# Block products for graph convolution: fewer PSUM banks per set of seven, partial sums copied out between the products

## The chip, the cores and the metric

The kernel runs on one core of a Trainium2 chip. The metric is device time in microseconds (us). The kernel before takes 2972.11 us, the median of three runs (2971.57 to 2972.21).

The engines are named as the profile names them. PE is TensorE, which multiplies matrices into PSUM; PEld is its loading of weights. DVE is VectorE, ACT is ScalarE and POOL is GpSimd. PSUM has eight banks here, each of 128 partitions by 512 float32 values. GpSimd works on SBUF tiles only in this kernel.

## The reference, cut to what matters

There are 64 graphs of 256 nodes with 512 features. Layer 0 is three graph convolutions, with a residual and a layer norm. Layer 1 is an attention without a full score matrix: one score for each node, a softmax over the nodes, and again a residual and a layer norm.

```python
# layer 0, for each graph
h = relu(adj @ (x @ W1) + b1)
h = relu(adj @ (h @ W2) + b2)
x = layernorm(x + adj @ (h @ W3) + b3)
# layer 1
q, k = split(x @ Wqk);  v = x @ Wv
agg = adj @ (k * mask)
w = mask * sum(q * agg, -1) / sqrt(512)
x = layernorm(x + softmax(w over nodes) * v)
```

Everything is float32.

## The kernel before

The kernel works on pairs of graphs (32 pairs). It has two streams of work that are emitted in turn: `front` does the first two convolutions of pair i, `back` the third convolution and the attention of pair i-1. `back` has more steps than `front`, so the last part of `back` is emitted when `front` of that turn has ended.

Most products (the three of features by weights, two with the adjacency, and one for each graph in the attention) use a scheme with seven block products in place of eight. Operands are cut into 2 x 2 blocks; sums and differences of blocks are made first, seven products are formed, and the four result blocks are sums of these. The products are numbered: 1 to 4 use plain blocks on at least one side, 5, 6 and 7 use sums on both. In the attention, q and k are folded into one matrix, M = Wq Wk^T, made once at the start.

The function that runs one set of seven:

```python
def seven(mm, c11, c12, c21, c22, shape, add11=None, plus=None):
    a = bank(shape)
    mm(1, a, True)                  # True: the first product in this bank
    t1 = tmp()...                   # [cut: a reshape]
    nc.scalar.copy(t1, a)           # ScalarE
    yield
    b = bank(shape)
    mm(6, b, True)
    u = tmp()...
    add(u, b, t1)                   # VectorE
    if plus is not None:            # only where the residual is added
        u12, u21, u22 = (tmp()... for _ in range(3))
        padd(u22, u, plus[2])       # GpSimd
        padd(u12, u, plus[0])
        padd(u21, u, plus[1])
    else:
        u12 = u21 = u22 = u
    yield
    c = bank(shape)
    mm(7, c, True)
    s7 = tmp()...
    add(s7, c, u22)
    yield
    d = bank(shape)
    mm(5, d, True)
    c22(d, s7)
    yield
    mm(2, a, False)                 # False: adds to what the bank holds
    c11(a)
    yield
    mm(3, d, False)
    c12(d, u12)
    yield
    mm(4, c, False)
    c21(c, u21)
    yield
```

Each `yield` hands the turn to the other stream. The sums of blocks of the features, made by GpSimd. `S[0]` goes to product 5, `S[1]` to 6, `S[2]` to 7, `S[3]` to 3:

```python
def a_sums(hT):                     # hT: four chunks of 128 features
    S = [pool.tile([P, 2, G, P], FP, name="S", tag="S", bufs=6) for _ in range(4)]
    blk = lambda h, c: hT[c][:, :, h * P:(h + 1) * P]
    sub = OP.subtract
    for c in range(2):
        padd(S[0][:, c], blk(1, c), blk(1, 2 + c))
    for c in range(2):
        padd(S[1][:, c], S[0][:, c], blk(0, c), sub)
    for c in range(2):
        padd(S[2][:, c], blk(0, c), blk(1, c), sub)
    for c in range(2):
        padd(S[3][:, c], blk(0, 2 + c), S[1][:, c], sub)
    ...                             # [cut: which source each product takes]
```

The features by weights (`support`), and the two streams:

```python
def support(hT, w):
    src = a_sums(hT)
    C = ...                         # [cut: four tiles for the result blocks]
    ...                             # [cut: mm(n, ps, first), 4 matmuls of 256 columns]
    yield from seven(mm, lambda a: nc.scalar.copy(C[0][0], a), lambda d, u: add(C[0][1], d, u),
                     lambda c, u: add(C[1][0], c, u), lambda d, u: add(C[1][1], d, u), (P, G, HD))
    return C

def front(i, hT, aT):
    C = yield from support(hT, wl[0])
    nxt = load_xT(i + 1) if i + 1 < NPAIR else None
    hT = yield from aggregate(C, aT, bcol[0])     # four steps, relu on ScalarE after each
    C = yield from support(hT, wl[1])
    hT = yield from aggregate(C, aT, bcol[1])
    return hT, nxt

def back(i, hT, aT, prev):
    # [cut: load of x, softmax and end of the pair before]
    C = yield from src                            # src = support(hT, wl[2])
    aS = adj_sums(aT)
    # [cut]
    yield from adj_times(aS, C, ..., plus=(xb(0, 1), xb(1, 0), xb(1, 1)))   # into r, with x
    for g in range(G):
        layernorm(r[:, g])
    yield 8
    # [cut: 16 transposes of r into x1T; mask times r into xm, on ScalarE]
    src = a_sums(x1T)
    # [cut: attention(g), a set of seven with products of 512 columns]
    yield from adj_times(aS, xmb, ...)            # into gt
    for g in range(G):
        yield from attention(g)
    return r, vs, w
```

`adj_times` makes four sums T of the other operand on GpSimd and then runs `seven` with products of two matmuls each. A float32 matmul shows as two records in the profile, so a product of `support` has eight records.

Of the kernel before, what the change touches and what calls it, by code (L numbers as in the profile page):

```python
# [20 lines left out]
def gcn_then_graph_attention(ctx: ExitStack, tc: tile.TileContext, xT, xN, adjT, mask, W1, b1, W2, b2, W3, b3,  # L21
# [29 lines left out]
    def bank(shape=(P, G, N)):  # L51
        return psum.tile(list(shape), FP, name="ps", tag="ps")

    def tmp():
        return pool.tile([P, D], FP, name="tmp", bufs=5)

    def add(o, a, b):
        nc.vector.tensor_tensor(o, a, b, op=OP.add)  # L58

    def padd(o, a, b, op=OP.add):  # L60
        nc.gpsimd.tensor_tensor(o, a, b, op=op)  # L61


    def load_xT(i):
        t = pool.tile([P, DC, G, N], FP, name="xT", bufs=1)
        nc.sync.dma_start(t, xT[i].rearrange("p (c g n) -> p c g n", c=DC, g=G))
        return [t[:, c] for c in range(DC)]

    def load_adj(i):
        t = pool.tile([P, NH, G, N], FP, name="aT", bufs=2)  # L70
# [17 lines left out]
    def halves(t, w):  # L88
        return t[:, :w], t[:, w:]

    def seven(mm, c11, c12, c21, c22, shape, add11=None, plus=None):

        a = bank(shape)
        mm(1, a, True)
        t1 = tmp().rearrange("p (a b) -> p a b", a=shape[1]) if len(shape) == 3 else tmp()
        nc.scalar.copy(t1, a)  # L96
        yield
        b = bank(shape)
        mm(6, b, True)
        u = tmp().rearrange("p (a b) -> p a b", a=shape[1]) if len(shape) == 3 else tmp()  # L100
        add(u, b, t1)
        if plus is not None:
            u12, u21, u22 = (tmp().rearrange("p (a b) -> p a b", a=shape[1]) for _ in range(3))
            padd(u22, u, plus[2])
            padd(u12, u, plus[0])
            padd(u21, u, plus[1])
        else:
            u12 = u21 = u22 = u
        yield
        c = bank(shape)  # L110
        mm(7, c, True)
        s7 = tmp().rearrange("p (a b) -> p a b", a=shape[1]) if len(shape) == 3 else tmp()
        add(s7, c, u22)
        yield
        d = bank(shape)
        mm(5, d, True)
        c22(d, s7)
        yield
        mm(2, a, False)
        c11(a)  # L120
        yield
        mm(3, d, False)
        c12(d, u12)
        yield
        mm(4, c, False)
        c21(c, u21)
        yield


# [38 lines left out]
    def make_m():  # L168

        qk = []  # L170
        for name, w, tag, in (("q", WqT, "act"), ("k", WkT, "sup")):
            qk.append([])
            for d in range(DC):
                t = pool.tile([P, D], FP, name=f"w{name}T", tag=tag, bufs=7)
                nc.sync.dma_start(t, w[d * P:(d + 1) * P, :])
                qk[-1].append(t)
        m = [const.tile([P, 2, D], FP, name=f"m{k}") for k in range(2)]
        v0 = pool.tile([P, 2, D], FP, name="v0", tag="v", bufs=3)
        nc.sync.dma_start(v0, Wv[:HD].rearrange("(c p) f -> p c f", p=P))
        v1 = const.tile([P, 2, D], FP, name="v1")  # L180
        nc.sync.dma_start(v1, Wv[HD:].rearrange("(c p) f -> p c f", p=P))
        yield
        for f in range(DC):
            pt = bank((P, D))
            for d in range(DC):
                nc.tensor.matmul(pt, lhsT=qk[0][d][:, f * P:(f + 1) * P], rhs=qk[1][d],
                                 start=(d == 0), stop=(d == DC - 1))
            nc.scalar.copy(m[f // 2][:, f % 2, :], pt)
            yield
        ts = [const.tile([P, 2, D], FP, name=f"mv_{s}") for s in KEYS]  # L190
        b_sums((m[0], v0, m[1], v1), ts, nc.gpsimd)
        mv.update({1: m[0], 2: m[1], 3: v1, 4: ts[3], 5: ts[0], 6: ts[1], 7: ts[2]})
        yield


    def a_sums(hT):

        S = [pool.tile([P, 2, G, P], FP, name="S", tag="S", bufs=6) for _ in range(4)]
        blk = lambda h, c: hT[c][:, :, h * P:(h + 1) * P]
        sub = OP.subtract  # L200
        for c in range(2):
            padd(S[0][:, c], blk(1, c), blk(1, 2 + c))
        for c in range(2):
            padd(S[1][:, c], S[0][:, c], blk(0, c), sub)
        for c in range(2):
            padd(S[2][:, c], blk(0, c), blk(1, c), sub)
        for c in range(2):
            padd(S[3][:, c], blk(0, 2 + c), S[1][:, c], sub)
        src = {1: lambda c, g: blk(0, c)[:, g], 2: lambda c, g: blk(0, 2 + c)[:, g],
               4: lambda c, g: blk(1, 2 + c)[:, g]}  # L210
        for n, s in ((5, 0), (6, 1), (7, 2), (3, 3)):
            src[n] = lambda c, g, s=s: S[s][:, c, g]
        return src

    def support(hT, w):

        src = a_sums(hT)
        C = [[pool.tile([P, G, HD], FP, name="sup", tag="sup", bufs=7) for _ in range(2)] for _ in range(2)]

        def mm(n, ps, first):  # L220
            for g in range(G):
                for c in range(2):
                    nc.tensor.matmul(ps[:, g], lhsT=src[n](c, g), rhs=w[n][:, c], start=(first and g == 0 and c == 0),  # L223
                                     stop=(g == G - 1 and c == 1), skip_group_check=True)
        yield from seven(mm, lambda a: nc.scalar.copy(C[0][0], a), lambda d, u: add(C[0][1], d, u),
                         lambda c, u: add(C[1][0], c, u), lambda d, u: add(C[1][1], d, u), (P, G, HD))
        return C

    def aggregate(C, aT, b):

        hT = []
        for c in range(DC):
            ps = bank()
            for g in range(G):
                for k in range(NH):
                    nc.tensor.matmul(ps[:, g], lhsT=C[k][c // 2][:, g, (c % 2) * P:(c % 2 + 1) * P],  # L236
                                     rhs=aT[:, k, g], start=(g == 0 and k == 0), stop=(g == G - 1 and k == NH - 1),
                                     skip_group_check=True)
            t = pool.tile([P, G, N], FP, name="hT", tag="act", bufs=7)
            nc.scalar.activation(t, ps, AF.Relu, bias=b[:, c:c + 1])  # L240
            hT.append(t)
            yield
        return hT

# [10 lines left out]
    def adj_times(aS, B, c11, c12, c21, c22, plus=None):  # L255

        Ts = [pool.tile([P, G, HD], FP, name="T", tag="T", bufs=4) for _ in range(4)]
        b_sums((B[0][0], B[0][1], B[1][0], B[1][1]), Ts, nc.gpsimd)
        mov = {1: B[0][0], 2: B[1][0], 3: B[1][1], 4: Ts[3], 5: Ts[0], 6: Ts[1], 7: Ts[2]}

        def mm(n, ps, first):
            for g in range(G):
                nc.tensor.matmul(ps[:, g], lhsT=aS[n][:, g], rhs=mov[n][:, g], start=(first and g == 0),  # L263
                                 stop=(g == G - 1), skip_group_check=True)
        yield from seven(mm, c11, c12, c21, c22, (P, G, HD), plus=plus)

    def stats(src):

# [50 lines left out]
    def back(i, hT, aT, prev):  # L319
# [10 lines left out]
        if prev is not None:  # L330
            s = softmax_cols(sm)
            for g in range(G):
# [3 lines left out]
        r = pool.tile([P, G, NH, D], FP, name="r", bufs=2)  # L336
        xb = lambda h, j: x[:, :, h, j * HD:(j + 1) * HD]
        rb = lambda h, j: r[:, :, h, j * HD:(j + 1) * HD]
        yield from adj_times(aS, C, lambda a: add(rb(0, 0), a, xb(0, 0)), lambda d, u: add(rb(0, 1), d, u),
                             lambda c, u: add(rb(1, 0), c, u), lambda d, u: add(rb(1, 1), d, u),  # L340
                             plus=(xb(0, 1), xb(1, 0), xb(1, 1)))
        for g in range(G):
            layernorm(r[:, g])
        yield 8
        x1T = []
        for c in range(DC):
            pt = bank()
            for g in range(G):
                for h in range(NH):
                    nc.tensor.transpose(pt[:, g, h * P:(h + 1) * P], r[:, g, h, c * P:(c + 1) * P], ident)  # L350
            t = pool.tile([P, G, N], FP, name="x1T", bufs=4)
            if c % 2:
                nc.vector.tensor_copy(t, pt)
            else:
                nc.scalar.copy(t, pt)
            x1T.append(t)
        yield
        xm = pool.tile([P, G, NH, D], FP, name="xm", tag="x", bufs=1)
        for h in range(NH):
# [10 lines left out]
        def attention(g):  # L370
# [10 lines left out]
                nc.vector.scalar_tensor_tensor(prod, y, mask_s[:, h, b:b + 1], gt[:, h, g, :], op0=OP.mult,  # L381
                                               op1=OP.mult, accum_out=w[:, h, g:g + 1])

            def c21(c, u):
                y = tmp()
                add(y, c, u)
                score(y, 1)
            vs[g] = v
            yield from seven(mm, lambda a: score(a, 0), lambda d, u: add(v[:, 0, :], d, u), c21,
                             lambda d, u: add(v[:, 1, :], d, u), (P, D))  # L390
        yield from adj_times(aS, xmb, lambda a: nc.scalar.copy(gb(0, 0), a), lambda d, u: add(gb(0, 1), d, u),
                             lambda c, u: add(gb(1, 0), c, u), lambda d, u: add(gb(1, 1), d, u))
        for g in range(G):
            yield from attention(g)
        return r, vs, w
# [79 lines left out]
```

## Time and profile before

| | |
|---|---|
| median of three runs | 2972.11 us |
| span of the profiled run | 2969.8 us |
| ScalarE busy | 623.7 us (21%) |
| GpSimd busy | 1413.6 us (48%) |
| one sum S of 128x256 on GpSimd | 0.73 us |
| one sum T of 128x512 on GpSimd | 1.27 us |
| one copy of a bank by ScalarE | 0.58 us |
| one addition of a bank by VectorE | 0.69 us |
| granted TensorE clock, mean | 0.994 |

An engine's busy time is the union of the stretches in which it ran something. An idle stretch is put down to the instruction, on whatever engine, whose end let the waiting one start. In the lists below, a group reads: line of the kernel, engine, operation, tile written <- tiles read, shape, count. A group's times are its busy time, the mean of one, and the idle time before it with its releasers. A line number can be that of a helper: L58 is VectorE's addition, L61 GpSimd's, L96 the copy of `t1`, L223 the matmuls of `support`, L236 those of `aggregate`, L263 those of `adj_times`, L376 those of the attention.

### The profile page before, as it was taken

The page shows a single profiled execution, that of the slowest core. Times are in us where ns is not written, and L with a number is a line of the kernel's source. Part 1 is how long each engine was busy: PE and PEld are TensorE (multiplying, and loading weights), DVE is VectorE, ACT ScalarE, POOL GpSimd, SP SyncE. Part 2 cuts the span into 40 slices and gives each one's busy share as a digit, 9 for nine tenths or more (in the row PEclk, how much of TensorE's full clock was granted, in tenths as well). Part 3 has the DMA queues.
Part 4 walks back from the last instruction along what each step waited for, and adds up shares of the span by engine and source line. Part 5 has one row for each costly group of instructions (what it writes and reads, how often), then busy time and mean ns, then how long its engine had stood idle before and what let it go on. Part 6 is the DMA issues. An engine that isn't in the chain of part 4 may idle for free. (4 is left out here: it accounts for less than half of the span.)

```text
span 2969.8 us, 30813 instructions
## 1 busy us (share of the span) xinstructions
PE 2882.4 (97%) x11680; PEld 2156.5 (73%) x11680; DVE 1356.8 (46%) x2638; ACT 623.7 (21%) x1062; POOL 1413.6 (48%) x1642
## 2 busy tenths in 40 slices
PE   7999999999999999999999999999999999999996
PEld 5877777777778777777777787777777777877774
DVE  2344544444444445444444444454444444444545
ACT  1212222212222122222122221222121222211221
POOL 5445455344554454554445544545544455445452
PEclk8999999999999999999999999999999999999998
DMA  4001011011011010110110110101101101101000
GB/s 146 31 34 50 26 46 50 29 50 50 22 50 49 31 50 29 43 50 29 50 50 22 50 50 29 50 30 41 50 29 50 50 22 50 50 29 50 33 17 29
DMA packets 28724, 126.04 MB, mean 42 GB/s; under 512 B 3232, under 2 KB 6432, under 8 KB 20384
## 3 DMA queue, kind: packets, MB, share of 16 engines
q1 hardware_dynamic: 28576, 124.08, 11.4%
q8 instruction: 92, 1.51, 0.2%
q14 instruction: 56, 0.46, 0.0%
HBM read 90.51 MB, written 33.55 MB: 42 GB/s over the span
## 5 line engine op out<-in xcount | busy, mean ns | idle before, releaser
L58 DVE TENSOR_TENSOR tmp<-ps,tmp 128x512 f32<-128x512 f32 x512 | 353.4, 690 | 693.9 <-PE ps L376 281.3
L223 PE MATMUL ps<-w_T,S 128*128 128x256 f32 x2304 | 538.1, 383 | 50.3 <-POOL S L61 50.2
L223 PEld LDWEIGHTS ps<-w_T,S 128*128 128x128 f32 x2304 | 434.4, 191 | 122.0 <-POOL S L61 63.1
L236 PE MATMUL ps<-aT,sup 128*128 128x256 f32 x2048 | 473.8, 381 | 0.0
L236 PEld LDWEIGHTS ps<-aT,sup 128*128 128x128 f32 x2048 | 386.4, 190 | 61.8 <-DVE sup L58 10.6
L376 PE MATMUL ps<-mv_T,S 128*128 128x512 f32 x768 | 340.0, 592 | 0.0
L96 ACT COPY tmp<-ps 128x512 f32<-128x512 f32 x224 | 130.3, 581 | 922.7 <-PE ps L376 464.7
L58 DVE TENSOR_TENSOR sup<-ps,tmp 128x512 f32<-128x512 f32 x288 | 194.4, 684 | 221.5 <-PE ps L223 116.6
L240 ACT ACTIVATE hT<-ps,b 128x512 f32<-128x512 f32 x256 | 175.9, 687 | 548.9 <-PE ps L236 548.9
L376 PEld LDWEIGHTS ps<-mv_T,S 128*128 128x128 f32 x768 | 145.9, 190 | 183.7 <-issue 160.7
L61 POOL TENSOR_TENSOR S<-hT 128x256 f32<-128x256 f32 x256 | 181.7, 725 | 204.7 <-PE ps L223 171.8
L83 POOL TENSOR_TENSOR T<-sup 128x512 f32<-128x512 f32 x32 | 40.6, 1269 | 426.2 <-DVE sup L58 426.2
L223 PE MATMUL ps<-w,hT 128*128 128x256 f32 x1024 | 242.0, 379 | 0.0
L376 PE MATMUL ps<-m,x1T 128*128 128x512 f32 x512 | 240.6, 592 | 0.0
L223 PEld LDWEIGHTS ps<-w,hT 128*128 128x128 f32 x1024 | 192.1, 190 | 25.7 <-issue 0.3
L83 POOL TENSOR_TENSOR T<-xm 128x512 f32<-128x512 f32 x32 | 40.8, 1274 | 326.9 <-ACT xm L362 320.1
L263 PE MATMUL ps<-T,aS 128*128 128x256 f32 x768 | 187.8, 381 | 1.4 <-POOL T L84 1.4
L275 ACT ACTIVATE sd<-mv,eps 128x2 f32<-128x2 f32 x128 | 34.5, 292 | 701.6 <-DVE mv L273 701.6
L223 PE MATMUL ps<-w,S 128*128 128x256 f32 x768 | 181.3, 379 | 0.1
L376 PEld LDWEIGHTS ps<-m,x1T 128*128 128x128 f32 x512 | 97.3, 190 | 108.8 <-issue 107.2
L61 POOL TENSOR_TENSOR S<-xT 128x256 f32<-128x256 f32 x128 | 90.8, 731 | 167.3 <-PE ps L376 160.7
L263 PEld LDWEIGHTS ps<-T,aS 128*128 128x128 f32 x768 | 146.8, 191 | 22.1 <-POOL T L84 1.8
(93 smaller groups left out, 3932.1 us busy)
## 6 DMA issues: line engine op xcount, KB each, us to landing
xT<-in_xT SPq DMA_DIRECT2D x32, 1024.0 KB, 4.9
x<-in_xN SPq DMA_DIRECT2D x32, 1024.0 KB, 4.9
out<-v SPq DMA_DIRECT2D x64, 512.0 KB, 2.6
aT<-in_adjT SPq DMA_DIRECT2D x32, 512.0 KB, 5.4
w<-in_W SPq DMA_DIRECT2D x9, 256.0 KB, 5.3
wqT<-in_WqT SPq DMA_DIRECT2D x4, 256.0 KB, 5.2
wkT<-in_WkT SPq DMA_DIRECT2D x4, 256.0 KB, 5.0
v<-in_Wv SPq DMA_DIRECT2D x2, 512.0 KB, 6.4
```

Of the source, the lines that this page charges most:

```text
L58: nc.vector.tensor_tensor(o, a, b, op=OP.add)
L61: nc.gpsimd.tensor_tensor(o, a, b, op=op)
L83: eng.tensor_tensor(Ts[0], B[1], B[0], op=sub)
L96: nc.scalar.copy(t1, a)
L223: nc.tensor.matmul(ps[:, g], lhsT=src[n](c, g), rhs=w[n][:, c], start=(first and g == 0 and c == 0), stop=(g == G - 1 and c == 1), skip_gr ...
L236: nc.tensor.matmul(ps[:, g], lhsT=C[k][c // 2][:, g, (c % 2) * P:(c % 2 + 1) * P], rhs=aT[:, k, g], start=(g == 0 and k == 0), stop=(g == ...
L240: nc.scalar.activation(t, ps, AF.Relu, bias=b[:, c:c + 1])
L263: nc.tensor.matmul(ps[:, g], lhsT=aS[n][:, g], rhs=mov[n][:, g], start=(first and g == 0), stop=(g == G - 1), skip_group_check=True)
L275: nc.scalar.activation(sd, mvt[:, :, 1], AF.Sqrt, bias=eps)
L376: nc.tensor.matmul(ps, lhsT=src[n](c, g), rhs=mv[n][:, c], start=(first and c == 0), stop=(c == 1), skip_group_check=True)
```

## The change: three banks, copies between the products, sums of half the features

What it does:

- `seven` takes its products in the order 1, 7, 6, 2, 5, 3, 4 and uses three banks, x, v and y. Products 1, 6, 5 and 3 gather in x: after 1, after 6 and after 5 ScalarE copies what the bank holds, and the next product is added on top. Products 7 and 4 gather in v; product 2 has y for itself. What VectorE added before now comes out of the gathering in the bank, so VectorE has two additions fewer in a set and ScalarE two copies more.
- The hidden features lie in two tiles of two chunks instead of four of one, so GpSimd makes each of the four sums in one instruction of 128x512. `S[2]` is made first: it needs the first two chunks only.
- x is added to three of the partial sums at other points of the set: one after product 1, two after product 5.
- The four copies of x1T are all on ScalarE; before, two of them were on VectorE.
- In the attention the blocks of v come first and those of M second, and M is made by matmuls of 128 columns in place of 512.
- The scratch tiles become six in place of five.

It is for taking work off VectorE and banks out of use, and for having the first needed sum early.

```diff
-    def seven(mm, c11, c12, c21, c22, shape, add11=None, plus=None):
-        [cut: the body shown above]
+    def seven(mm, shape, c11, c12, c21, c22, plus=None):
+        x = bank(shape)
+        mm(1, x, True)
+        t1 = shaped(shape)
+        nc.scalar.copy(t1, x)
         if plus is not None:
+            padd(t1, t1, plus[0])
+        yield
+        v = bank(shape)
+        mm(7, v, True)
+        yield
+        mm(6, x, False)
+        u = shaped(shape)
+        nc.scalar.copy(u, x)
+        yield
+        y = bank(shape)
+        mm(2, y, True)
+        c11(y, t1)
+        yield
+        mm(5, x, False)
+        q = shaped(shape)
+        nc.scalar.copy(q, x)
+        if plus is not None:
+            padd(q, q, plus[2])
+            padd(u, u, plus[1])
+        c22(v, q)
+        yield
+        mm(3, x, False)
+        c12(x)
+        yield
+        mm(4, v, False)
+        c21(v, u)
         yield
 ...
         for f in range(DC):
             pt = bank((P, D))
             for d in range(DC):
-                nc.tensor.matmul(pt, lhsT=qk[0][d][:, f * P:(f + 1) * P], rhs=qk[1][d],
-                                 start=(d == 0), stop=(d == DC - 1))
+                for j in range(DC):
+                    nc.tensor.matmul(pt[:, j * P:(j + 1) * P], lhsT=qk[0][d][:, f * P:(f + 1) * P],
+                                     rhs=qk[1][d][:, j * P:(j + 1) * P], start=(d == 0 and j == 0),
+                                     stop=(d == DC - 1), skip_group_check=True)
             nc.scalar.copy(m[f // 2][:, f % 2, :], pt)
 ...
-        b_sums((m[0], v0, m[1], v1), ts, nc.gpsimd)
-        mv.update({1: m[0], 2: m[1], 3: v1, 4: ts[3], 5: ts[0], 6: ts[1], 7: ts[2]})
+        b_sums((v0, m[0], v1, m[1]), ts, nc.gpsimd)
+        mv.update({1: v0, 2: v1, 3: m[1], 4: ts[3], 5: ts[0], 6: ts[1], 7: ts[2]})
 ...
-        for c in range(2):
-            padd(S[0][:, c], blk(1, c), blk(1, 2 + c))
-        for c in range(2):
-            padd(S[1][:, c], S[0][:, c], blk(0, c), sub)
-        for c in range(2):
-            padd(S[2][:, c], blk(0, c), blk(1, c), sub)
-        for c in range(2):
-            padd(S[3][:, c], blk(0, 2 + c), S[1][:, c], sub)
+        padd(S[2], blk(0, 0), blk(1, 0), sub)
+        padd(S[0], blk(1, 0), blk(1, 1))
+        padd(S[1], S[0], blk(0, 0), sub)
+        padd(S[3], blk(0, 1), S[1], sub)
 ...
-        yield from seven(mm, lambda a: nc.scalar.copy(C[0][0], a), lambda d, u: add(C[0][1], d, u),
-                         lambda c, u: add(C[1][0], c, u), lambda d, u: add(C[1][1], d, u), (P, G, HD))
+        yield from seven(mm, (P, G, HD), lambda y, t: add(C[0][0], y, t), lambda x: nc.scalar.copy(C[0][1], x),
+                         lambda v, t: add(C[1][0], v, t), lambda v, t: add(C[1][1], v, t))
 ...
-            t = pool.tile([P, G, N], FP, name="x1T", bufs=4)
-            if c % 2:
-                nc.vector.tensor_copy(t, pt)
-            else:
-                nc.scalar.copy(t, pt)
-            x1T.append(t)
+            nc.scalar.copy(x1T[c // 2][:, c % 2], pt)
 ...
-            yield from seven(mm, lambda a: score(a, 0), lambda d, u: add(v[:, 0, :], d, u), c21,
-                             lambda d, u: add(v[:, 1, :], d, u), (P, D))
+            yield from seven(mm, (P, D), lambda y, t: add(v[:, 0, :], y, t), lambda x: score(x, 0),
+                             lambda ps, t: add(v[:, 1, :], ps, t), c22)
```

The score of the second half of the nodes is taken in `c22` now, after product 5, where it was in `c21`, after product 4. The sums for r and gt are passed in the same new form. The features' tiles (`hT`, `x1T`, `xT`) are indexed by half.

More of the change, by code (lines that the diff above doesn't have):

```diff
@@ L54, in tmp @@
     def tmp():
-        return pool.tile([P, D], FP, name="tmp", bufs=5)
+        return pool.tile([P, D], FP, name="tmp", bufs=6)
     def add(o, a, b):
@@ L66, in load_xT @@
         nc.sync.dma_start(t, xT[i].rearrange("p (c g n) -> p c g n", c=DC, g=G))
-        return [t[:, c] for c in range(DC)]
+        return [t[:, :2], t[:, 2:]]
     def load_adj(i):
@@ L89, in halves, with shaped @@
         return t[:, :w], t[:, w:]
-    def seven(mm, c11, c12, c21, c22, shape, add11=None, plus=None):
[L93 to L96, printed above, removed]
-        yield
[L98 to L101, printed above, removed]
-        if plus is not None:
[L103 to L106, printed above, removed]
-        else:
-            u12 = u21 = u22 = u
+    def shaped(shape):
+        t = tmp()
+        return t.rearrange("p (a b) -> p a b", a=shape[1]) if len(shape) == 3 else t
+    def seven(mm, shape, c11, c12, c21, c22, plus=None):
[5 more added lines that the diff above has]
+            padd(t1, t1, plus[0])
+        yield
+        v = bank(shape)
[12 more added lines that the diff above has]
+        nc.scalar.copy(q, x)
+        if plus is not None:
+            padd(q, q, plus[2])
+            padd(u, u, plus[1])
+        c22(v, q)
         yield
[L110 to L113, printed above, removed]
+        mm(3, x, False)
+        c12(x)
         yield
[L115 to L126, printed above, removed]
+        mm(4, v, False)
+        c21(v, u)
         yield
@@ L170, in make_m @@
         qk = []
-        for name, w, tag, in (("q", WqT, "act"), ("k", WkT, "sup")):
+        for name, w in (("q", WqT), ("k", WkT)):
             qk.append([])
             for d in range(DC):
-                t = pool.tile([P, D], FP, name=f"w{name}T", tag=tag, bufs=7)
+                if name == "k":
+                    t = pool.tile([P, D], FP, name="wkT", tag="sup", bufs=7)
+                elif d % 2 == 0:
+                    two = pool.tile([P, 2, D], FP, name="wqT", tag="act", bufs=5)
+                    t = two[:, 0]
+                else:
+                    t = two[:, 1]
                 nc.sync.dma_start(t, w[d * P:(d + 1) * P, :])
                 qk[-1].append(t)
-        m = [const.tile([P, 2, D], FP, name=f"m{k}") for k in range(2)]
-        v0 = pool.tile([P, 2, D], FP, name="v0", tag="v", bufs=3)
+        m = [pool.tile([P, 2, D], FP, name="m0", tag="v", bufs=3), const.tile([P, 2, D], FP, name="m1")]
+        v0 = const.tile([P, 2, D], FP, name="v0")
         nc.sync.dma_start(v0, Wv[:HD].rearrange("(c p) f -> p c f", p=P))
@@ L198, in a_sums @@
         S = [pool.tile([P, 2, G, P], FP, name="S", tag="S", bufs=6) for _ in range(4)]
-        blk = lambda h, c: hT[c][:, :, h * P:(h + 1) * P]
+        blk = lambda h, k: hT[k][:, :, :, h * P:(h + 1) * P]
         sub = OP.subtract
-        for c in range(2):
-            padd(S[0][:, c], blk(1, c), blk(1, 2 + c))
-        for c in range(2):
-            padd(S[1][:, c], S[0][:, c], blk(0, c), sub)
-        for c in range(2):
-            padd(S[2][:, c], blk(0, c), blk(1, c), sub)
-        for c in range(2):
-            padd(S[3][:, c], blk(0, 2 + c), S[1][:, c], sub)
[L209 to L213, printed above, removed]
+        padd(S[2], blk(0, 0), blk(1, 0), sub)
+        padd(S[0], blk(1, 0), blk(1, 1))
+        padd(S[1], S[0], blk(0, 0), sub)
+        padd(S[3], blk(0, 1), S[1], sub)
+        src = {1: blk(0, 0), 2: blk(0, 1), 4: blk(1, 1), 5: S[0], 6: S[1], 7: S[2], 3: S[3]}
+        return {n: (lambda c, g, t=t: t[:, c, g]) for n, t in src.items()}
     def support(hT, w):
@@ L224, in mm @@
                                      stop=(g == G - 1 and c == 1), skip_group_check=True)
-        yield from seven(mm, lambda a: nc.scalar.copy(C[0][0], a), lambda d, u: add(C[0][1], d, u),
-                         lambda c, u: add(C[1][0], c, u), lambda d, u: add(C[1][1], d, u), (P, G, HD))
+        yield from seven(mm, (P, G, HD), lambda y, t: add(C[0][0], y, t), lambda x: nc.scalar.copy(C[0][1], x),
+                         lambda v, t: add(C[1][0], v, t), lambda v, t: add(C[1][1], v, t))
         return C
     def aggregate(C, aT, b):
-        hT = []
+        hT = [pool.tile([P, 2, G, N], FP, name="hT", tag="act", bufs=5) for _ in range(2)]
         for c in range(DC):
@@ L238, in aggregate @@
                                      skip_group_check=True)
-            t = pool.tile([P, G, N], FP, name="hT", tag="act", bufs=7)
-            nc.scalar.activation(t, ps, AF.Relu, bias=b[:, c:c + 1])
-            hT.append(t)
+            nc.scalar.activation(hT[c // 2][:, c % 2], ps, AF.Relu, bias=b[:, c:c + 1])
             yield
@@ L264, in mm @@
                                  stop=(g == G - 1), skip_group_check=True)
-        yield from seven(mm, c11, c12, c21, c22, (P, G, HD), plus=plus)
+        yield from seven(mm, (P, G, HD), c11, c12, c21, c22, plus=plus)
     def stats(src):
@@ L338, in back @@
         rb = lambda h, j: r[:, :, h, j * HD:(j + 1) * HD]
-        yield from adj_times(aS, C, lambda a: add(rb(0, 0), a, xb(0, 0)), lambda d, u: add(rb(0, 1), d, u),
-                             lambda c, u: add(rb(1, 0), c, u), lambda d, u: add(rb(1, 1), d, u),
-                             plus=(xb(0, 1), xb(1, 0), xb(1, 1)))
+        yield from adj_times(aS, C, lambda y, t: add(rb(0, 0), y, t), lambda x: add(rb(0, 1), x, xb(0, 1)),
+                             lambda v, t: add(rb(1, 0), v, t), lambda v, t: add(rb(1, 1), v, t),
+                             plus=(xb(0, 0), xb(1, 0), xb(1, 1)))
         for g in range(G):
@@ L344, in back @@
         yield 8
-        x1T = []
+        x1T = [pool.tile([P, 2, G, N], FP, name="x1T", tag="act", bufs=5) for _ in range(2)]
         for c in range(DC):
@@ L350, in back @@
                     nc.tensor.transpose(pt[:, g, h * P:(h + 1) * P], r[:, g, h, c * P:(c + 1) * P], ident)
-            t = pool.tile([P, G, N], FP, name="x1T", bufs=4)
-            if c % 2:
-                nc.vector.tensor_copy(t, pt)
-            else:
-                nc.scalar.copy(t, pt)
-            x1T.append(t)
+            nc.scalar.copy(x1T[c // 2][:, c % 2], pt)
         yield
@@ L382, in score, with c22 @@
                                                op1=OP.mult, accum_out=w[:, h, g:g + 1])
-            def c21(c, u):
+            def c22(ps, t):
                 y = tmp()
-                add(y, c, u)
+                add(y, ps, t)
                 score(y, 1)
             vs[g] = v
-            yield from seven(mm, lambda a: score(a, 0), lambda d, u: add(v[:, 0, :], d, u), c21,
-                             lambda d, u: add(v[:, 1, :], d, u), (P, D))
-        yield from adj_times(aS, xmb, lambda a: nc.scalar.copy(gb(0, 0), a), lambda d, u: add(gb(0, 1), d, u),
-                             lambda c, u: add(gb(1, 0), c, u), lambda d, u: add(gb(1, 1), d, u))
+            yield from seven(mm, (P, D), lambda y, t: add(v[:, 0, :], y, t), lambda x: score(x, 0),
+                             lambda ps, t: add(v[:, 1, :], ps, t), c22)
+        yield from adj_times(aS, xmb, lambda y, t: add(gb(0, 0), y, t), lambda x: nc.scalar.copy(gb(0, 1), x),
+                             lambda v, t: add(gb(1, 0), v, t), lambda v, t: add(gb(1, 1), v, t))
         for g in range(G):
```

## The prediction

> **What bounds the kernel now.** I read the page's busy line first, then what TensorE waited for, then the order of time of one pair of graphs in the middle of the run.
>
> ```profile
> PE 2882.4 (97%) x11680; PEld 2156.5 (73%) x11680; DVE 1356.8 (46%) x2638; ACT 623.7 (21%) x1062; POOL 1413.6 (48%) x1642
> ```
>
> TensorE is busy for 97% and no other engine for half. The change takes no matrix product away, so all it can win is TensorE's idle time. What that engine waited for (who it waited for: us in total, times, longest):
>
> ```profile
> PE ps L223 <- POOL S L61: 50.2, 32, 4.6
> PE ps L186 <- DMA wkT<-in_WkT: 6.9, 1, 6.9
> PE ps L223 <- DMA w<-in_W: 6.8, 1, 6.8
> PE ps L350 <- DVE r L283: 4.2, 1, 4.2
> ```
>
> One wait repeats: 32 times, once a pair, on the block sums S that GpSimd makes of the hidden features. The longest, 4.6, is the first pair's; the others come to (50.2 - 4.6) / 31 = 1.47 us. The rest happens once, at the start or the end. In order of time, TensorE in one pair (start, duration, line, what, count, idle before it):
>
> ```profile
> 1019.87 1.89 PE L223 MATMUL ps<-w,hT 128*128 128x256 f32 x8
> 1021.59 1.03 PE L263 MATMUL ps<-sup,aT 128*128 128x256 f32 x4
> 1022.46 0.59 PE L223 MATMUL ps<-w_T,S 128*128 128x256 f32 x2
> 1024.52 1.56 PE L223 MATMUL ps<-w_T,S 128*128 128x256 f32 x6 [1.47 <-POOL S L61]
> 1025.92 1.03 PE L263 MATMUL ps<-sup,aS 128*128 128x256 f32 x4
> ```
>
> From starts, a support product takes 1.72 us (1019.87 to 1021.59), an adjacency product of half the matmuls 0.87. Two of the eight records of the second support product ran; the next should have started at 1022.46 + 2 x 0.216 = 1022.89 and started at 1024.52. So 1.63 us are lost per pair (the printed 1.47 leaves out 0.16 by which the modelled end of a matmul outlasts its slot). GpSimd before that moment:
>
> ```profile
> 1015.73 3.72 POOL L61 TENSOR_TENSOR tmp<-tmp,x 128x512 f32<-128x512 f32 x3 [1.43 <-DVE tmp L58]
> 1019.40 0.73 POOL L61 TENSOR_TENSOR S<-hT 128x256 f32<-128x256 f32 x1
> 1020.21 0.73 POOL L61 TENSOR_TENSOR S<-S,hT 128x256 f32<-128x256 f32 x1
> 1020.89 1.41 POOL L61 TENSOR_TENSOR S<-hT 128x256 f32<-128x256 f32 x2
> 1022.26 0.73 POOL L61 TENSOR_TENSOR S<-hT,S 128x256 f32<-128x256 f32 x1
> 1022.94 0.73 POOL L61 TENSOR_TENSOR S<-hT 128x256 f32<-128x256 f32 x1
> 1023.75 0.72 POOL L61 TENSOR_TENSOR S<-S,hT 128x256 f32<-128x256 f32 x1
> ```
>
> Three additions of x to partial sums hold GpSimd until 1019.4; then seven sums of 128x256 pass before S[1] of the second chunk is there (1024.47). Product 6, second in the order, needs it.
>
> **What the Trainium skill says.** Perfetto Trace Analysis, "Identifying the Most-Contended Engine", warns that matmul busy share is no measure of headroom. Here spacing settles it: 216 ns for 256 columns, 430 for 512, without gaps outside the wait above, so the stream is full. The same page, "Matmuls", advises rotating independent groups through different PSUM banks so that evacuation overlaps the next group. The change goes against that: products 1, 6, 5 and 3 share one bank, with a copy between each two. ScalarE: Activation LUTs, "What ACT_TABLE_LOAD costs", gives 186 ns + 0.833 ns per element, an estimate of 612 ns for 512; the copies in this trace take 581, so the trace's figure is used. TensorE: Matmul & The Clock Gate, "Back-to-back issue gap", gives 81 ns for matmuls of 128 columns with weight loads against 56 alone; no stream of that shape runs in this trace.
>
> **Part 1, the sums.** Eight sums of 128x256 at 0.73 us (5.8 us) become four of 128x512. GpSimd's operations of that size (T<-sup, x<-x,b3b) take 1.27, so 5.1 us. More important is the order: product 7 comes second and needs only S[2], made of the first half of the features, and two of the three x-additions move behind product 5. On the clock of the profile: the four T sums end near 1014.3, the one x-addition left near 1015.6, S[2] near 1016.9, against a product at 1022.46. S[0] and S[1] wait for the last relu (1019.95) and end near 1022.5; product 6 now stands at 1025.05. The wait goes, with some 2.5 us of slack: 31 x 1.63 = 51 us, and about 3 of the first pair's 4.6 (there GpSimd also makes the sums of the attention weights, so I leave some).
>
> **Part 2, evacuation.** Counting instructions per pair: ScalarE gets 16 more copies (two in each of seven sets of products, two for x1T), 16 x 0.58 = 9.3 us; VectorE loses 16 of 0.69, 11 us. That makes ScalarE about 624 + 297 = 921 us (31%), VectorE about 1357 - 353 = 1004 (34%). Neither is near TensorE, so the totals are worth nothing by themselves.
>
> **Part 3, the new waits on bank x.** A relu or copy starts 0.26 us after the writer's slot ends (1019.00 to 1019.26, ScalarE on hT; likewise 1021.59 to 1021.84), takes 0.58, and TensorE restarts 0.05 after its releaser (1024.47 to 1024.52). So a bank is closed for about 0.88 us after its slot. Products 1 and 6 have product 7 between them, 6 and 5 have product 2: 0.87 or 1.72 us, just enough. Between 5 and 3 there is nothing of the same set. While front and back alternate, the other supplies a product. But front's second support runs alone while back waits for its layer norm, and gt and both attention sets run after front is done: four bare gaps per pair. Unfilled that is 4 x 0.88 = 3.5 us per pair, 109 us over 31. Against it: the emitted order isn't program order; later ready work is pulled forward. In the kernel before, front's product 4 overtakes back's product 3:
>
> ```profile
> 1004.33 1.46 PE L223 MATMUL ps<-w_T,xT 128*128 128x256 f32 x6
> 1005.62 1.89 PE L223 MATMUL ps<-w,S 128*128 128x256 f32 x8
> 1007.35 0.59 PE L223 MATMUL ps<-w_T,xT 128*128 128x256 f32 x2
> 1007.78 1.89 PE L223 MATMUL ps<-w_T,hT 128*128 128x256 f32 x8
> ```
>
> Each bare gap has such work ready: product 1 of attention(0), of attention(1), of the next pair's support, and the first halves of the aggregation. I let fill all but a fifth through: 0.7 us per pair, 22 us.
>
> The bank v is also reopened: product 4 waits for the addition of 7 to 5. In the adjacency set with x that is copy 0.84, GpSimd 1.27, VectorE 0.69, near 3.0 us after product 5, plus queueing behind S[3]; on the shifted clock the addition ends at 1025.8, and product 4 stands at 1026.8. Hidden, with 1 us to spare.
>
> **Part 4, start and end.** M = Wq Wk^T goes from 32 matmul records of 512 columns (430 ns, 13.8 us) to 128 of 128 columns. At the 216-ns rate scaled that is 109 ns each, no change; with the page's 81/56 it is an estimate of 158 ns, 20.2 us, so +6. TensorE is full in that stretch, so it counts. In the last pair back runs alone and its gaps have little filler, +3; the last score now follows product 3, not 4, so the softmax hides a product (1.72) and an addition (0.69), -2.4.
>
> **Sum.** -51 - 3 + 22 + 6 + 1 = -25 us: 2972 - 25 = 2947.
>
> **Rivals.** (a) The gaps stay bare: -51 - 3 + 109 + 6 + 1 = +62, 3034 us. For it: in the tail TensorE stands idle in spite of reordering (1.56, 1.04 and 1.39 us for ScalarE, VectorE and GpSimd), and the very stall of 1.63 shows that the order chosen trusted GpSimd to be faster than it was. Against: filler is long, 0.43 to 0.86 us per matmul, and exists in each gap. (b) Every gap is filled and the weight loads hide: -51 - 3 - 1, about 2917. This is nearly the floor; what else TensorE idles is start and end. (c) The wait for S moves: GpSimd's queue is strict, so an x-addition waiting for a copy could hold S back, or the six S buffers could be freed too late. For it: GpSimd already waits 247.7 us for attention matmuls to free S. Against: those waits end 2 us and more before use. Half the gain lost: about 2970. (d) ScalarE's strict queue: a square root of the layer norm, waiting for VectorE, sits ahead of a copy that TensorE needs. Up to 1 us per pair, about 2975.
>
> **Range and chances.** Gain and gaps are of like size and opposite sign, so the middle is a small gain. The range runs from (b) to halfway between (d) and (a): 2915 to 3000. Faster by over 2% needs 59 us, more than the repeated wait holds: 0.04. Slower by over 2% needs all gaps bare: 0.09. Within 2%: 0.87.
>
> **What would show it.** Right: the 32 waits of support matmuls for POOL S gone or one; TensorE's busy time near 2880; POOL near 1320 us, ACT near 920, DVE near 1005; attention products no longer in order set by set. Wrong: TensorE waiting for the ScalarE copies at the new line in seven, 60 to 130 times with 0.5 to 0.9 us each (gaps bare); waits for additions of v; a start longer by over 10 us (weight loads).

## The result, and the profile after

The changed kernel takes 2920.93 us, the median of four runs (2920.62 to 2922.45), beside 2972.16 us for the kernel before on the same chip. The ratio is 0.9829, with a 95% interval from 0.9812 to 0.9846: 51 us less, where 25 were predicted.

The busy line of the page after:

```profile
PE 2883.0 (99%) x11776; PEld 2150.7 (74%) x11776; DVE 1009.2 (35%) x2126; ACT 911.4 (31%) x1574; POOL 1346.4 (46%) x1130
```

TensorE is as busy as before, 2883 us, in a span that is 51 us shorter. VectorE lost 348 us and ScalarE gained 288, and neither is what the span follows. What TensorE waits for after (who it waited for: us in total, times, longest):

```profile
PE ps L227 <- DMA w<-in_W: 6.7, 1, 6.7
...
PE ps L373 <- ACT tmp L119: 1.4, 2, 0.7
```

The wait for POOL S, 32 times before, has left the list. The wait for ScalarE's third copy in a set (L119), which bare gaps were to show 60 to 130 times, comes four times in all, twice in this line and once each in two smaller ones, all from 2835 us on.

To see where the 51 us lie, take the first transposes of r in the first and in the last but one turn of `back`, 30 pairs apart (the view in order of time; start, duration, line, what). Before:

```profile
136.52 1.91 PE L350 MATMUL ps<-ident,r 128*128 128x128 f32 x16
...
2857.09 1.91 PE L350 MATMUL ps<-ident,r 128*128 128x128 f32 x16
```

After:

```profile
124.90 1.91 PE L352 MATMUL ps<-ident,r 128*128 128x128 f32 x16
...
2806.02 1.91 PE L352 MATMUL ps<-ident,r 128*128 128x128 f32 x16
```

| | before | after | difference |
|---|---|---|---|
| start, up to the first transposes | 136.5 | 124.9 | -11.6 |
| 30 pairs, each | 90.69 | 89.37 | -1.32 (x30: -39.4) |
| end, from the last but one | 112.7 | 112.8 | +0.1 |

So a pair gains 1.32 us, less than the 1.63 that was read for the wait, and the start gains as much as nearly nine pairs.

How a gap between products 5 and 3 looks after, in attention, on TensorE:

```profile
1033.51 1.88 PE L373 MATMUL ps<-mv_T,S 128*128 128x512 f32 x4
1035.22 1.02 PE L373 MATMUL ps<-v,x1T 128*128 128x512 f32 x2
1036.15 1.95 PE L373 MATMUL ps<-m,S 128*128 128x512 f32 x4
```

The first line is product 5 of attention(0) and the third product 3. Between them stand two records of product 1 of attention(1), 0.86 us of work. Product 3 starts 0.93 after them, so the gap costs 0.07 us and not 0.9.

### The profile page after: what moved, and what is told of

The parts are those of the page before. It is cut to its first block, busy times and chain, and to the rows that moved or that the text cites. A ratio compares the mean times of both kernels' runs of the same rounds, so it can differ in the third digit from the quotient of the medians.

```text
span 2918.8 us, 30346 instructions
## 1 busy us (share of the span) xinstructions
PE 2883.0 (99%) x11776; PEld 2150.7 (74%) x11776; DVE 1009.2 (35%) x2126; ACT 911.4 (31%) x1574; POOL 1346.4 (46%) x1130
## 5 line engine op out<-in xcount | busy, mean ns | idle before, releaser
L227 PE MATMUL ps<-w_T,S 128*128 128x256 f32 x2304 | 524.0, 379 | 2.2 <-DVE w_T L85 1.6
L240 PE MATMUL ps<-aT,sup 128*128 128x256 f32 x2048 | 484.0, 381 | 0.0
L373 PE MATMUL ps<-mv_T,S 128*128 128x512 f32 x768 | 350.5, 592 | 0.0
L111 ACT COPY tmp<-ps 128x512 f32<-128x512 f32 x224 | 131.3, 586 | 523.9 <-PE ps L227 290.8
L102 ACT COPY tmp<-ps 128x512 f32<-128x512 f32 x224 | 130.2, 581 | 401.4 <-PE ps L227 212.0
L119 ACT COPY tmp<-ps 128x512 f32<-128x512 f32 x224 | 130.7, 584 | 399.1 <-PE ps L373 180.5
L373 PE MATMUL ps<-v,x1T 128*128 128x512 f32 x512 | 251.0, 592 | 0.0
L61 POOL TENSOR_TENSOR S<-hT 128x512 f32<-128x512 f32 x128 | 162.5, 1270 | 144.7 <-PE ps L373 104.7
L58 DVE TENSOR_TENSOR v<-ps,tmp 128x512 f32<-128x512 f32 x128 | 88.5, 691 | 405.5 <-PE ps L373 405.5
L58 DVE TENSOR_TENSOR gt<-ps,tmp 128x512 f32<-128x512 f32 x96 | 66.4, 692 | 414.2 <-PE ps L265 388.6
L58 DVE TENSOR_TENSOR r<-ps,tmp 128x512 f32<-128x512 f32 x96 | 65.3, 680 | 407.6 <-PE ps L265 270.5
L265 PE MATMUL ps<-T,aS 128*128 128x256 f32 x768 | 197.0, 386 | 3.5 <-POOL T L85 3.5
```

What stands on the lines that cost most here:

```text
L102: nc.scalar.copy(t1, x)
L111: nc.scalar.copy(u, x)
L119: nc.scalar.copy(q, x)
L373: nc.tensor.matmul(ps, lhsT=src[n](c, g), rhs=mv[n][:, c], start=(first and c == 0), stop=(c == 1), skip_group_check=True)
```

## The experiments

All times below are medians; the ratio is to the kernel before on the same chip, with its 95% interval. "Start" and "pair" are read from the first transposes, as in the table above.

| kernel | us | ratio | start | pair |
|---|---|---|---|---|
| e1: half-feature sums alone | 2921.98 | 0.9835 (0.9820 to 0.9849) | 128.7 | 89.23 |
| e2: the rest of the change alone | 2918.00 | 0.9824 (0.9809 to 0.9838) | 125.0 | 89.25 |
| e3: x-additions to VectorE alone | 2919.43 | 0.9823 (0.9807 to 0.9839) | 134.6 | 88.96 |
| e4: after, one gap bare | 2948.42 | 0.9923 (0.9908 to 0.9938) | 123.7 | 90.23 |
| e5: after, M by 512 columns | 2920.26 | 0.9831 (0.9816 to 0.9845) | 124.7 | 89.37 |
| e6: before, six banks | 2970.23 | 0.9999 (0.9991 to 1.0008) | 135.5 | 90.68 |
| e7: after, five banks | 2942.31 | 0.9906 (0.9892 to 0.9921) | 125.0 | 90.06 |
| e10: product 7 before 6 alone | 2915.44 | 0.9817 (0.9801 to 0.9833) | 128.1 | 88.95 |
| e8: e10 and half-feature sums | 2913.70 | 0.9805 (0.9791 to 0.9818) | 126.2 | 88.94 |
| e9: e8 and x-additions to VectorE | 2914.13 | 0.9805 (0.9791 to 0.9818) | 127.7 | 88.94 |
| after, beside e8 and e9 | 2921.10 | 0.9828 (0.9814 to 0.9841) | 123.7 | 89.37 |

### Which part takes the wait away: e1, e2, e3, e10

**e1**, only the sums, on the kernel before (the layout of `hT`, `x1T`, `xT` and `wqT` follows):

```diff
-        for c in range(2):
-            padd(S[0][:, c], blk(1, c), blk(1, 2 + c))
-        ...                          # 8 sums of 128x256
+        padd(S[0], blk(1, 0), blk(1, 1))
+        padd(S[1], S[0], blk(0, 0), sub)
+        padd(S[2], blk(0, 0), blk(1, 0), sub)
+        padd(S[3], blk(0, 1), S[1], sub)
```

> The kernel before with one part of the change: features in two tiles, four sums of 128x512 in place of eight of 128x256, in the old order S[0], S[1], S[2], S[3]; the seven products as before. Theory A (the wait for S is a matter of how late S[1] is, however it is made earlier): GpSimd is held by the x-additions to 1019.4 of the old clock, S[0] starts at the last relu (1019.95) and S[1] ends near 1022.5, where product 6 stands at 1022.46; nearly all of the 1.63 us per pair goes, near 2922 us. Rival B (the gain is the new order of products and x-additions, the size of a sum doesn't matter): at most a third of the gain, 2955 us or more.

2921.98 us. The repeated wait is gone; the sums end just in time, with 0.2 us of it left in each pair.

**e2**, the change without that part:

```diff
-        padd(S[2], blk(0, 0), blk(1, 0), sub)
-        ...                          # 4 sums of 128x512
+        for o, p, q, op in (...):    # the same four, S[2] first
+            for c in range(2):
+                padd(S[o][:, c], p(c), q(c), op)
```

> The changed kernel with its sums cut again into eight of 128x256, S[2] still first; the new order of products and x-additions stays. Theory A: product 7 needs S[2] only, and product 6 has 2.6 us more, so no wait for S comes back: 2921 us, within 4. Rival (fewer and longer sums are what made S early): a wait of 0.5 to 1.5 us per pair comes back, 2935 to 2970 us.

2918.00 us: as fast as the whole change. Half-feature sums add nothing that can be measured to the rest.

**e3**, three words in the kernel before:

```diff
-            padd(u22, u, plus[2])
-            padd(u12, u, plus[0])
-            padd(u21, u, plus[1])
+            add(u22, u, plus[2])
+            add(u12, u, plus[0])
+            add(u21, u, plus[1])
```

> The kernel before with nothing changed but that VectorE makes the three additions of x. Theory Q (GpSimd's queue is the cause: three additions of 1.27 us stand ahead of the sums): the first chunk's sums run before the last relu, S[1] of the second chunk ends near 1019.95 + 2 x 0.73 = 1021.4, before product 6 at 1022.46; the wait of 1.63 us per pair goes, 2922 us. Rival (eight small sums are too many, whatever stands ahead): at least half the wait stays, 2945 us or more.

2919.43 us. GpSimd in one pair of this kernel, the first and the seventh of its sums, in order of time:

```profile
1000.19 0.73 POOL L61 TENSOR_TENSOR S<-hT 128x256 f32<-128x256 f32 x1 [3.14 <-PE ps L263]
...
1004.54 0.72 POOL L61 TENSOR_TENSOR S<-S,hT 128x256 f32<-128x256 f32 x1
```

GpSimd now sits idle for 3.14 us before the first sum, where the three additions stood. That sum begins 5.02 us ahead of product 6, where it began 3.06 ahead of it before (1019.40 and 1022.46). S[1] of the second chunk ends at 1005.26, and product 6, whose third record at 1005.64 is the first to read it, runs without a wait:

```profile
1004.34 1.03 PE L263 MATMUL ps<-sup,aT 128*128 128x256 f32 x4
1005.21 1.89 PE L223 MATMUL ps<-w_T,S 128*128 128x256 f32 x8
```

**e10**, only the order, on the kernel before:

```diff
+        c = bank(shape)
+        mm(7, c, True)
+        yield
         b = bank(shape)
         mm(6, b, True)
         ...                          # u, x-additions as before
-        yield
-        c = bank(shape)
-        mm(7, c, True)
         s7 = ...
         add(s7, c, u22)
```

and in `a_sums` the two lines of S[2] come first.

> The kernel before with product 7 ahead of product 6 and S[2] made first; sums small, x-additions and copies as before. Theory A (any shift of more than 1.6 us between the sums and the product that needs them is enough): the x-additions end at 1019.4 of the old clock, S[2] near 1020.9, S[1] near 1023.8 against product 6 at 1025.05: the wait goes, 2921 us. Rival (GpSimd's queue, not the order, decides): product 7 waits in place of product 6, 2940 us or more.

2915.44 us, the lowest of the four, though the intervals of their ratios overlap. GpSimd and then TensorE in one pair:

```profile
995.98 3.73 POOL L61 TENSOR_TENSOR tmp<-tmp,x 128x512 f32<-128x512 f32 x3
...
1000.46 0.72 POOL L61 TENSOR_TENSOR S<-S,hT 128x256 f32<-128x256 f32 x1
```

```profile
1001.29 1.89 PE L223 MATMUL ps<-w_T,S 128*128 128x256 f32 x8
```

The x-additions still stand ahead of the second chunk's S[0] and S[1] on GpSimd, but S[1] ends at 1001.18 and product 6 starts only at 1001.29, behind product 7. So the additions (e3), the number of the sums (e1) and the order of two products (e10), each changed alone, take the same wait away; e3 and e10 need a few lines only. The stall was 1.63 us deep, and each moves the sums or their use by about that or more; done together they can't add. e10 keeps VectorE busy for 1349.3 us and has four banks a set, so neither the relief of VectorE nor the fewer banks is needed for the gain.

### What the shared bank costs: e4, e7, e6

**e4**, the changed kernel with the filler of one gap held back. The added line changes no value; it ties product 1 of attention(1) to the first score of attention(0):

```diff
             v = pool.tile([P, NH, D], FP, name="v", tag="v", bufs=3)
+            if g == 1:
+                e = x1T[0][:, 0, 1, 0:1]
+                nc.vector.scalar_tensor_tensor(e, w[:, 0, 0:1], 0.0, e, op0=OP.mult, op1=OP.add)
```

> The changed kernel with one element of x1T of the second graph rewritten by VectorE (as 0 times the first graph's score plus itself), so that product 1 of attention(1) can't be pulled into the gap between products 5 and 3 of attention(0). All else stays, and the values too. Theory F (later work fills the gaps): TensorE waits for the ScalarE copy in that gap, 0.83 us in place of 0.15 lost, once a pair: +0.7 x 32 = +22 us, 2943 us. Rival (the gap is short anyway, because the copy ends before TensorE has drained): no change, 2921 us.

2948.42 us, 27.5 more than the changed kernel: 0.86 per pair. The gap in order of time, TensorE and then ScalarE:

```profile
1040.93 1.88 PE L376 MATMUL ps<-mv_T,S 128*128 128x512 f32 x4
1043.58 1.96 PE L376 MATMUL ps<-m,S 128*128 128x512 f32 x4 [0.77 <-ACT tmp L119]
```

```profile
1042.85 0.58 ACT L119 COPY tmp<-ps 128x512 f32<-128x512 f32 x1 [2.79 <-PE ps L376]
```

Product 5's slot ends at 1040.93 + 1.72 = 1042.65. The copy starts 0.20 later and ends at 1043.43, and product 3 starts 0.15 after that: 0.93 us bare, beside 0.07 filled. An estimate from this one gap: four of this size would cost 3.7 us per pair, which with e10's 88.95 makes 92.7, beside 90.69 for the kernel before. By it, filling is what keeps this scheme from a loss.

**e7**, the changed kernel with five banks (`bufs=5` in the PSUM pool):

> The changed kernel with five PSUM banks in place of eight. If filling the gaps between products 5 and 3 needs free banks for the work pulled forward, and five are too few, TensorE waits for ScalarE's copies again: up to 4 x 0.8 us per pair, 2950 to 3020 us. If three banks a set leave enough for filler even so, 2921 us, within 5.

2942.31 us, 21 more; per pair 90.06 beside 89.37. Neither theory fits: the loss is below the range of the first, and it lies elsewhere. The gaps between 5 and 3 are still filled. What comes back is a wait of product 4, on the bank that 7 and 5 are added from: it starts 0.58 us late, at 1080.23 in place of 1079.65. TensorE in this kernel, then in the changed one at the same place:

```profile
1079.22 0.59 PE L240 MATMUL ps<-aT,sup 128*128 128x256 f32 x2
1080.23 1.99 PE L227 MATMUL ps<-w_T,xT 128*128 128x256 f32 x8 [0.42 <-DVE sup L58]
```

```profile
1072.25 0.59 PE L240 MATMUL ps<-aT,sup 128*128 128x256 f32 x2
1072.68 0.59 PE L265 MATMUL ps<-sup,aT 128*128 128x256 f32 x2
1073.11 1.89 PE L227 MATMUL ps<-w_T,xT 128*128 128x256 f32 x8
```

With eight banks two pieces of later work stand before product 4; with five, one. Nothing but the number of banks was changed, so the second lacks a bank; which product holds it is not shown.

**e6**, the kernel before with six banks:

> The kernel before with six PSUM banks in place of eight. If banks were scarce before and the three-bank scheme gains by that, this is slower by 1% or more (over 3000 us). If banks were never what TensorE waited for, it stays at 2972, within 6 us.

2970.23 us, ratio 0.9999. Two banks fewer cost the kernel before nothing, so banks weren't what it lacked.

### The start: e5

**e5**, the changed kernel with the 16 matmuls of 512 columns for M:

> The changed kernel with M made by 512-column matmuls again. The prediction's theory (short matmuls are held up by their weight loads, 158 ns in place of 109): 6 us less, 2915 us. Rival, from the trace after (64 records from 31.59 to 38.74, 112 ns each): the loads hide, 128 x 112 against 32 x 430 ns is 0.6 us, so 2920 us.

2920.26 us, beside 2920.93 and 2921.10 for the changed kernel: the rival holds. In the changed kernel the 64 records of the second half run as

```profile
31.59 7.31 PE L196 MATMUL ps<-wkT,wqT 128*128 128x128 f32 x64
38.74 1.46 PE L227 MATMUL ps<-w,S 128*128 128x256 f32 x6
```

(38.74 - 31.59) / 64 = 0.112 us each. A weight load for each matmul of 128 columns is all but hidden.

### The best of both: e8, e9

**e8** is e10 with the half-feature sums: the kernel before's four banks and its VectorE additions, product 7 ahead of 6, S[2] first. **e9** puts the x-additions on VectorE as well, as e3 does.

> The kernel before with its four banks and VectorE additions, but half-feature sums, S[2] first, and product 7 ahead of product 6; x-additions still on GpSimd. If ScalarE's copies out of the bank cost about 0.3 us per pair in restarts of TensorE (1.0 us per pair lost after, 0.6 in the kernel with x-additions on VectorE) and give nothing back, this is faster than the changed kernel: 2921 - 31 x 0.35 = 2910 us. If the copies are themselves part of the gain: 2921 us or more.

> The same, with the three x-additions on VectorE. Theory: the wait for S is gone already, so nothing more comes of it per pair: 2910 us, within 3 of the kernel without that. Rival (the additions still delay what TensorE needs): 5 us or more faster.

> The changed kernel itself on the same chip as the two above, for comparison: 2921 us, within 3.

2913.70 and 2914.13 us, against 2921.10 for the changed kernel on that chip. e8 is faster than both kernels, by 58 and by 7 us; the 2910 expected of it was 4 too low. A pair takes 88.94 in place of 89.37, and 30 x 0.43 = 12.9 us come of that. The changed kernel's start on that chip is 2.5 us shorter (123.7 beside 126.2), and from the last but one transposes on e8 takes 2911.8 - 2794.4 = 117.4 us, 3.0 more than the changed kernel there (114.4). 12.9 - 2.5 - 3.0 leaves 7.4. The changed kernel's own start and end differ by 1.2 and 1.6 us between its two profiles, so little hangs on differences of that size there; its pair is 89.37 in both. That moving the x-additions adds nothing was expected of e9.

Where the 0.43 lie can be read from the starts of TensorE's records in one pair. By as much as they lie further apart than 0.216 us (256 columns) or 0.430 (512), the changed kernel loses 0.99 us and e8 0.57. Of the difference, 0.22 is lost in attention, 0.14 at product 3 of the second support and 0.06 in the set for gt, where the changed kernel restarts in bank x. That the shared bank causes it all is read from these places, not tested apart.

## Why the prediction was right or wrong

**The bound and the wait: right.** The repeated wait on S was the gain, it went whole, and no wait of its size took its place. The reason given for it, the x-additions ahead of the sums on GpSimd, is shown by e3; e1 and e10 show that what counts is how late the sums are for the product that reads them, whichever of the two is moved. One detail was wrong: of the two x-additions that I put behind product 5, one still runs ahead of S[0] in the trace after (at 1084.38, S[0] at 1086.17). The slack covered it.

**"31 x 1.63 = 51 us": a little small.** A pair of e3 and of e10 is 1.73 and 1.74 us shorter than before. The missing 0.10 comes just behind the wait: the second record after it starts 0.32 us after the first, in place of 0.216.

**"I let fill all but a fifth through: 0.7 us per pair": mis-sized.** The changed kernel's pair is 0.42 us longer than e10's (89.37 and 88.95): several restarts of 0.07 to 0.08. A bare gap is 0.93 us (0.88 was worked out), and the later work that fills it is in the right place in every pair up to the last turns. I had taken the stalls of the kernel before as a sign that the order would miss; they were waits for GpSimd, and these are for ScalarE. Why the order fits the one and not the other stays open. With the 0.11 of the wait, 0.28 makes 0.39 per pair, 31 x 0.39 = 12 us of the 26 that the prediction fell short.

**"with the page's 81/56 it is an estimate of 158 ns, 20.2 us, so +6": wrong.** The ratio of the Trainium skill (TensorE: Matmul & The Clock Gate, "Back-to-back issue gap") does not carry over to these float32 matmuls: 112 ns each, and e5, with 512 columns, is less than 1 us faster. That makes 6 us. The trace before could have told: the 16 transposes have this shape, with a weight load each, though the prediction says that no such stream runs there.

```profile
1043.37 1.91 PE L350 MATMUL ps<-ident,r 128*128 128x128 f32 x16
1045.12 1.03 PE L263 MATMUL ps<-xm,aT 128*128 128x256 f32 x4
```

From start to start they take 1.75 us, 0.109 each.

**"about 3 of the first pair's 4.6": mis-sized.** Before, the second support of the first pair (TensorE, then the stretch behind the wait, where the third figure from the end is the granted clock):

```profile
53.30 0.59 PE L223 MATMUL ps<-w_T,S 128*128 128x256 f32 x2
58.53 7.84 PE L223 MATMUL ps<-w_T,S 128*128 128x256 f32 x22 [4.63 <-POOL S L61]
```

```profile
58.50:66.20 7.70, 7.67 (x22) 6.29 (x23) 1.38 (x2) 0.00 (x0) 3.54 (x5) 0.62 0.00 0
```

The wait lost 4.8 us from start to start, and then 22 records took 7.7 us where 22 x 0.216 = 4.75 would have done, at a granted clock of 0.62. The Trainium skill says on the same page ("What's actually happening") that an idle window of about 3.4 us throttles TensorE to half its clock; the trace agrees, with 0.50 from 58.5 to 63.8 us and near full clock from 64.2 on. So this one wait cost some 7.7 us. After, this support runs at full clock:

```profile
48.85 1.89 PE L227 MATMUL ps<-w,hT 128*128 128x256 f32 x8
```

```profile
48.80:62.30 13.50, 13.49 (x63) 11.34 (x62) 1.38 (x2) 3.03 (x5) 8.78 (x7) 1.00 0.00 0
```

Besides, product 1 of this support starts at 48.85 in place of 51.57. In the trace after, 34 records of the first support run before the weights for M have landed, beside 24 before, and TensorE idles 1.2 us for these weights in place of 6.9; the prediction left that out, and no run tests it apart.

**The end: right.** +1 was predicted and +0.1 came, though the end differs by 1.6 us between two profiles of the changed kernel.

With the terms as measured: 30 pairs of 1.32 (39.4), the start 11.6 (1.6 from the regular wait among it, some 7.3 of the first pair's wait and 2.7 of the earlier products), the end -0.1: 51 us. The 26 us by which the prediction fell short are then 12 from the pairs, 6 from M, 7 from the rest of the start and 1 from the end. Rival (b), 2917 us, was the nearest, in part by luck: it counted no restarts (0.42 x 31 = 13 us), but also 7 us too little at the start and 3 too little of the wait, and these nearly cancel. It called itself nearly the floor; e8 shows 2914.

## What to carry to other kernels

Where one engine is full, look for the one wait that repeats and ask for its smallest cure first: here a change of order in a few lines gained as much as the whole rework, and cures of one stall didn't add. A chain of products through one PSUM bank with a copy between them was cheap here because independent work could be pulled into each gap, and that work needs banks: with five in place of eight, product 4 was left to wait, 0.58 us a pair. Count a stall of several microseconds on TensorE with what follows at the lower clock.

## What the runs showed of the hardware that was not expected

- Matmuls of 128 columns in float32 with a weight load each sustained one record in 0.112 us, beside 0.216 for 256 and 0.430 for 512 columns.
- After 4.6 us without work TensorE's granted clock was 0.50 for the next 5.3 us; over 7.7 us its mean was 0.62.
- In the bare gap of e4, 0.15 us passed from the end of ScalarE's copy to the restart of TensorE on that bank, and 0.20 from the end of the writing product's slot to the copy's start.
